# Where the first loads stand in an attention and mixture-of-experts kernel: weights loaded later, bias loads on another queue, and three PSUM banks in the first prologue

## The chip, the cores and the metric

The kernel runs on one core of a Trainium2 chip. The metric is the device time of one execution in microseconds (us); the time before is the median of three runs. One further execution was recorded by the profiler, and all times of single steps come from it.

## The reference

The input x has 8 batches of 1024 tokens with 256 features, all in float32. Two layers follow each other, each with a residual and a layer norm:

```
q, k, v = x Wq + bq, x Wk + bk, x Wv + bv               # 16 heads of 16
gate    = a (b c - 1) + 2,  a, b = sigmoid(sums of x gru_W + gru_b)
scores  = q k / 4 + gate[row] * rel_embed[bucket(col - row)][head]
x       = layernorm(x + softmax(scores) v Wo + bo)

p       = softmax(x Wr)                                  # 8 experts, best 2 per token
x       = layernorm(x + sum over the 2 experts of weight * ffn_e(x))
ffn(x)  = gelu(x W1 + b1) W2 + b2                        # 256 -> 1024 -> 256
```

An expert takes at most 2560 of the 8192 tokens, in their order; a token that meets a full expert goes through a fallback network instead.

## The kernel before

The program has two parts. The first does attention and routing for all batches, the second runs the experts over rows that the first part has scattered to DRAM. The change lies in the first part, before its main loop.

The main loop runs over units. A unit is a pair of heads of one batch, so there are 8 units per batch and 64 in all, with 16 steps each. A step takes 128 keys (j) and half of the queries (c): TensorE (PE) makes the scores, VectorE (DVE) adds the near part of the position bias, ScalarE (ACT) takes the exponential, and PE multiplies with v. To subtract a row's maximum beforehand, the kernel computes maxima of the scores in a pass of their own (`max_first`, `max_second`, `max_fold`), `LEAD` = 21 steps ahead of the scores. So 21 steps of maxima stand before the main loop: these are the "first maxima".

q and k are split into three bfloat16 parts each. `halves(b, xT, m)` does that for half m of the heads: for each half of the tokens a k projection and a q projection, four in all (four PE instructions each, called pq). ACT takes the first part out of PSUM (L626), DVE the remainder (L639), ACT the second part (L418), GpSimd (POOL) the third (L419), and a DMA on SyncE's queue stores the three to DRAM (`kd`, `qd`, L643; of k also differences, `dd`, L657). The SBUF tile `parts` has three buffers and is used by the gates too. `gating` computes the gates: two products pg, a bias added by DVE (z), a chain on ACT and POOL (g), two transposes pgt of it, and stores to `gd` and, in eight pieces each time, `fd` (L580, L591). `prologue` transposes x (pt, copied by ACT to xT, L468), starts `gating` and `halves(b, xT, 0)`, and makes v (pv). `load_unit` loads the parts of one unit back into ks, ks_d and qs: 19 DMAs per unit. `load_gates` loads a unit's gates (L965), which POOL multiplies with `bias` to `gb` (L985); `shift` stores a unit's maxima into qs (row, L1094).

These generators take turns in `streams`, a scheduler at build time: each says at a yield what it needs next. `BANK` takes the next entry of the list `banks`, a PSUM bank; after `HELD` or `SLOW` ACT or DVE reads that bank. Before the change the list has one entry, `(ps_x, "bank")`, until the last epilogue, where the banks `pm0` and `pm1` are added. These two otherwise hold the maxima.

The order of instructions on each engine has two regimes. From the line with `manual_schedule` (L393) on, each engine and queue takes them in the order in which the program states them. Before it a planner orders them by their readiness in its own estimate, and by their order in the program. So the tables and loads ahead of L393 need not run in the order of their lines.

The tables before the loop: from `embT` (the relative embeddings, transposed) DVE copies 79 pieces into `strip` (L318) and 79 into `back` (L325). `back` is stored to DRAM (`stripd`, L329), and one DMA of 4 MB spreads it to `blocks` (L332), from which each unit's `bias` is loaded (L950). DVE makes `strip16` from `strip`, stored as `stripb`, from which `biasb` is loaded (L929). `pattern` (ten loads) and zeros for `fd` (two stores of `zero`) come after them in the program.

The loads that the change touches: `heads_b` in DRAM gathers the small biases of k and q from five loads on ACT's queue; `bk_sb` and `bq_sb` are read back from it on ACT's queue (L230), and DVE scales `bq_sb` (L254). `later_weights`, called just before L393, loads on SyncE's (SP's) queue `wv_sb` (v projection), `wr_sb` (router), `bv_sb`, `bo_sb`, and `wo_sb` (output projection) in 16 pieces. The router's and the output projection's weights are read by `epilogue`, `bo_sb` by `add_bias`, all of it from batch 0's end on.

Of the kernel before, what the change touches and what calls it, by code (L numbers as in the profile page):

```python
# [11 lines left out]
F32 = mybir.dt.float32  # L12
# [4 lines left out]
ALU = mybir.AluOpType  # L17
# [4 lines left out]
P = 128  # L22
H, D = 16, 16
NG, HG = 4, 4
E = H * D
# [25 lines left out]
META = 5  # L51
# [27 lines left out]
def tile_attention_moe(  # L79
# [25 lines left out]
    nc = tc.nc  # L105
# [47 lines left out]
    with ExitStack() as at:  # L153
        cst = at.enter_context(tc.tile_pool(name="cst", bufs=1))
# [5 lines left out]
        ps_m = at.enter_context(tc.tile_pool(name="ps_m", bufs=1, space=PSUM))  # L160
        ps_x = at.enter_context(tc.tile_pool(name="ps_x", bufs=1, space=PSUM))
# [6 lines left out]
        banks = [(ps_x, "bank")]  # L168

        def bank(name):  # L170
            pool, tag = banks[0]
            banks.append(banks.pop(0))
            return pool.tile([P, CH], F32, tag=tag, name=name)
# [9 lines left out]
        def load_piece(b, n, tag="xp", bufs=3):  # L183

            xp = work.tile([P, 2, E], F32, tag=tag, name=f"xp{b}_{n}", bufs=bufs)
            nc.sync.dma_start(
                out=xp,
                in_=x[b, n * 2 * P : (n + 1) * 2 * P, :].rearrange(
                    "(t p) e -> p t e", p=P
                ),  # L190
            )
            return xp

        first_pieces = [load_piece(0, n) for n in range(3)]
        first_pieces.append(load_piece(0, 3, "rest", 2))


        emb = work.tile([NBUCKET, H], F32, tag="osb", name="emb", bufs=1)
        nc.sync.dma_start(out=emb, in_=rel)
# [2 lines left out]
            out=gb_ld.rearrange("p g o -> p (g o)"), in_=gru_b.to_broadcast([P, 8])  # L202
# [7 lines left out]
        bq_sb = cst.tile([P, NK], F32, name="bq_sb")  # L210
        bk_sb = cst.tile([P, NK], F32, name="bk_sb")
        for sb, src in ((wk_sb, wk), (wq_sb, wq)):
            for k in range(NK):
                nc.scalar.dma_start(
                    out=sb[:, k, :].rearrange("p (h d) -> p h d", d=D),
                    in_=src[k * P : (k + 1) * P, :].rearrange("p (h w) -> p h w", w=32)[
                        :, :, :D
                    ],
                )
        heads_b = dram.tile([2, H, D], F32, name="heads_b")  # L220
        nc.scalar.dma_start(
            out=heads_b[0], in_=kcl[8, :].rearrange("(h w) -> h w", w=32)[:, :D]
        )
        for g in range(H // HG):
            nc.scalar.dma_start(
                out=heads_b[1, g * HG : (g + 1) * HG, :],
                in_=bq[:, g].rearrange("(r w) -> r w", w=32)[:HG, :D],
            )
        for sb, which in ((bk_sb, 0), (bq_sb, 1)):
            nc.scalar.dma_start(  # L230
                out=sb,
                in_=heads_b[which].rearrange("h d -> (h d)").rearrange("(k p) -> p k", p=P),
            )
        wv_sb = cst.tile([P, NK, E], F32, name="wv_sb")
        wr_sb = cst.tile([P, NK, NE], F32, name="wr_sb")
        wo_sb = cst.tile([P, NK, E], F32, name="wo_sb")
# [1 line left out]
        bv_sb = cst.tile([P, E], F32, name="bv_sb")  # L238

        def later_weights():  # L240
            for sb, src in ((wv_sb, wv), (wr_sb, wr)):
                nc.sync.dma_start(out=sb, in_=src.rearrange("(k p) m -> p k m", p=P))
            nc.sync.dma_start(out=bv_sb, in_=bv.to_broadcast([P, E]))
            nc.sync.dma_start(out=bo_sb, in_=wo[D : D + 1, :].to_broadcast([P, E]))
            for h in range(H):
                k, r = divmod(h * D, P)
                nc.sync.dma_start(
                    out=wo_sb[r : r + D, k, :], in_=wo[h * 32 : h * 32 + D, :]
                )


        scale = 1.0 / math.sqrt(D)
        nc.vector.tensor_scalar(wq_sb, wq_sb, scale, None, ALU.mult)
        nc.vector.tensor_scalar(bq_sb, bq_sb, scale, None, ALU.mult)  # L254


        gs = cst.tile([P, 2], F32, name="gs")
# [8 lines left out]
        for base, sign in ((0, 1), (D - 1, -1)):  # L266
            nc.gpsimd.affine_select(
                out=wg, in_=wg, compare_op=ALU.is_ge, fill=0.0, base=base,
# [7 lines left out]
            out=anti, in_=anti, compare_op=ALU.not_equal, fill=1.0, base=-(P - 1),  # L276
# [7 lines left out]
            out=later, in_=later, compare_op=ALU.is_gt, fill=0.0, base=0,  # L284
# [5 lines left out]
            out=sel, in_=sel, compare_op=ALU.not_equal, fill=1.0, base=0,  # L290
# [32 lines left out]
        for lo, hi in zip(cuts[:-1], cuts[1:]):  # L323
# [9 lines left out]
            out=blocks,  # L333
            in_=bass.AP(
                sd.tensor, sd.offset + EDGE + 1 - REACH, [[STRIP, H], [-1, P], [1, WIN]]
            ),
# [15 lines left out]
        for side, bk in enumerate((int(farn[0]), int(far[0]))):  # L352
            nc.sync.dma_start(
                out=farb[:, side, :], in_=rel[bk : bk + 1, :].to_broadcast([P, H])
            )

        zero = cst.tile([P, 1, E + META], F32, name="zero")
        nc.gpsimd.memset(zero, 0.0)

        gd = [dram.tile([H, N], F32, name=f"gd{i}") for i in range(2)]  # L360
        qd = [dram.tile([3, E, N], BF16, name=f"qd{i}") for i in range(2)]
# [6 lines left out]
        for t in fd:  # L368
# [4 lines left out]
                out=flat, in_=zero16.unsqueeze(1).to_broadcast([P, flat.shape[1], 2 * E])  # L373
# [15 lines left out]
        o_acc = ps_o.tile([P, CH], F32, name="o_acc")  # L389
        nc.vector.memset(o_acc, 0.0)  # L390

        later_weights()
        at.enter_context(tc.manual_schedule())  # L393


        def clearing():
            for rows in (xd[:, :], yd[1:, :]):
                per, width = rows.shape[0] // P, rows.shape[1]
                spread = rows.rearrange("(p n) e -> p n e", p=P)
                for lo in range(0, per, 4):  # L400
                    n = min(4, per - lo)
                    nc.sync.dma_start(
                        out=spread[:, lo : lo + n, :],
                        in_=zero[:, :, :width].to_broadcast([P, n, width]),
                    )
                    for _ in range(4):
                        yield
            nc.sync.dma_start(out=yd[0:1, :], in_=zero[0:1, 0, :E])
# [46 lines left out]
        def prologue(b, pieces):  # L455
            me = batches[b]
            xT = once.tile([P, NK, N], F32, tag="xT", name=f"xT{b}")
            for n in range(NI // 2):
                yield BANK
                pt = bank("pt")  # L460
                ptv = pt.rearrange("p (k t n) -> p k t n", k=NK, t=2)
                for k in range(NK):
                    for t in range(2):
                        nc.tensor.transpose(
                            ptv[:, k, t, :], pieces[n][:, t, k * P : (k + 1) * P], ident
                        )
                yield HELD
                nc.scalar.copy(  # L468
                    xT[:, :, n * 2 * P : (n + 1) * 2 * P],
                    pt.rearrange("p (k n) -> p k n", k=NK),  # L470
                )
                if len(pieces) < NI // 2:
                    pieces.append(load_piece(b, len(pieces)))

            streams.start(gating(b, xT))
            yield from halves(b, xT, 0)


            v = perb.tile([P, NI, H, D + 1], F32, tag="v", name=f"v{b}")
            me.v = v  # L480
            nc.gpsimd.memset(v[:, :, :, D : D + 1], 1.0)
            for j in range(0, NI, 2):
                yield BANK
                pv = bank("pv")
                pvv = pv.rearrange("p (j e) -> p j e", j=2)
                for jj in range(2):
                    for k in range(NK):
                        nc.tensor.matmul(
                            pvv[:, jj, :],
                            xT[:, k, (j + jj) * P : (j + jj + 1) * P],  # L490
                            wv_sb[:, k, :],
                            start=(k == 0),
                            stop=(k == NK - 1),
                        )
                yield SLOW
                for jj in range(2):
                    nc.vector.tensor_tensor(
                        v[:, j + jj, :, 0:D],
                        pvv[:, jj, :].rearrange("p (h d) -> p h d", h=H),
                        bv_sb.rearrange("p (h d) -> p h d", h=H),  # L500
                        ALU.add,
                    )
            yield from halves(b, xT, 1)
# [552 lines left out]
        def max_second(m, common=False):  # L1056

            pm = bank("pm") if common else ps_m.tile([P, CH], F32, tag="pm0", name="pm0")
            half_scores(m, 0, pm)
            units[m // STEPS].rest = pm  # L1060
# [201 lines left out]
            load_max_bias(u)  # L1262
        load_bias(0)
        batches[0].rows, batches[0].gated = 0, False
        streams.start(prologue(0, first_pieces))
        while batches[0].rows < P or not batches[0].gated:
            streams.step()
# [1 line left out]
            nc.gpsimd.tensor_copy(t[R_FAR:], pattern[R_FAR:])  # L1269
        for t in KD:  # L1270
            nc.gpsimd.memset(t[R_FAR:], 0.0)
        clear = clearing()
        for u in range(2):
            for which in range(3):
# [4 lines left out]
        for m in range(LEAD):  # L1279
# [8 lines left out]
            streams.bank()  # L1288
            max_second(m)
        streams.drain()  # L1290
        for j in range(2):
            gate_biases(0, j)
        G = UNITS * STEPS
# [22 lines left out]
        for g in range(G + 12):  # L1316
            u, s = divmod(g, STEPS)
            j, c = divmod(s, NCH)
            b, sb = divmod(g, UB * STEPS)
            m = g + LEAD  # L1320
# [54 lines left out]
                take_outputs(u - 1)  # L1375
            next(clear, None)

        banks += [(ps_m, "pm0"), (ps_m, "pm1")]
        streams.start(epilogue(B - 1, batches[B - 1]))
        streams.drain()  # L1380

# [261 lines left out]
```

## Time and profile before

| | |
|---|---|
| median of three runs | 3657.59 us (3646.69 to 3658.37) |
| profiled execution | 3654.03 us, its span 3652.2 us |
| busy share of the span | PE 90%, POOL 61%, ACT 56%, DVE 53% |
| mean granted clock of PE | 0.963 |
| start of the first maximum (first L1025 on PE) | 101.04 us |
| start of the first scores of the main loop (L1109) | 140.03 us |
| PE busy from 0 to 101 us | 38.4 us |
| PE busy from 300 to 2426 us | 1991.7 us |

The span is the time from the first to the last instruction of the profiled execution; the execution's own time is 1.8 us longer. In a line of the order of time stand the start in us, the duration in us (of all instructions merged into the line), the engine, the line of the program, the operation, what it writes and reads, and the count; in brackets the idle time of the engine before it and what ended that. "SPq" and "ACTq" are the queues on which SP and ACT issue DMAs: the duration there is that of issuing, and the data lands later. A line of waits gives the waiting engine and line, whom it waited for, the total in us, how often, and the longest. A line of the stretches gives the stretch, its length, and the busy time of PE, PE's weight loads, DVE, ACT and POOL (in brackets the number of instructions), then PE's granted clock, the share of the DMA engines' time and GB/s.

### The profile page before, as it was taken

What the parts mean: (1) busy time and instruction counts of PE and PEld (TensorE: products, weight loads), DVE (VectorE), ACT (ScalarE), POOL (GpSimd) and SP (SyncE); (2) the same over time, 40 slices, a digit from 0 to 9 for tenths busy, and PEclk for the clock granted to TensorE, in tenths of its full rate; (3) what the DMA queues carried; (4) which work ended last, traced back from release to release, by engine and by line L of the source; (5) the groups of instructions that cost most, each with busy time, mean ns of one, the idle gap of its engine ahead of it and who ended that gap; (6) DMA issues with size and microseconds to landing.
All of it is one profiled execution on the core that took longest, in us unless ns stands there. A gap on an engine that the chain in (4) does not pass through costs nothing. (4 is left out here: it accounts for less than half of the span.)

```text
span 3652.2 us, 53430 instructions
## 1 busy us (share of the span) xinstructions
PE 3277.1 (90%) x16263; PEld 1655.8 (45%) x16263; DVE 1935.0 (53%) x5559; ACT 2047.8 (56%) x3084; POOL 2221.9 (61%) x2619
## 2 busy tenths in 40 slices
PE   4798998989999999999999999994399999999997
PEld 2342343334334334334334433333267677667776
DVE  2455656655765665665666576661134344444443
ACT  1577777767777777777787777771022222222222
POOL 2667666876886887787787788782233333333332
PEclk8899999999999999999999999995699999999999
DMA  5567657655643453444444444420332332232220
GB/s 139 159 167 196 190 167 192 186 177 177 186 146 111 139 155 114 130 141 135 125 135 137 133 135 129 132 92 10 113 88 58 88 90 67 85 96 88 72 90 21
DMA packets 380418, 455.71 MB, mean 125 GB/s; under 512 B 87478, under 2 KB 285235, under 8 KB 380107
## 3 DMA queue, kind: packets, MB, share of 16 engines
q1 hardware_dynamic: 338602, 388.06, 35.9%
q0 software_dynamic: 19296, 43.38, 4.2%
q10 hardware_dynamic: 22208, 20.58, 1.9%
q8 instruction: 138, 2.26, 0.3%
q14 instruction: 174, 1.42, 0.1%
HBM read 315.16 MB, written 140.54 MB: 125 GB/s over the span
## 5 line engine op out<-in xcount | busy, mean ns | idle before, releaser
L1131 ACT ACTIVATE pr<-sc 128x1024 f32<-128x1024 f32 x1024 | 1049.0, 1025 | 321.5 <-DVE sc L1124 298.9
L985 POOL TENSOR_TENSOR gb<-bias,gates 128x1024 f32<-128x1024 f32 (+2 forms) x512 | 1070.2, 2091 | 133.6 <-DMA gates<-gd 67.3
L1066 DVE CUSTOM_DVE_ANT_0 over<-pm,over 128x512 f32<-128x512 f32 x1024 | 703.8, 687 | 794.4 <-ACT over L1054 303.9
L1054 ACT ACTIVATE over<-pm 128x512 f32<-128x512 f32 x1024 | 612.7, 598 | 260.9 <-PE pm L1029 242.1
L1109 PE MATMUL sc<-qs,ks 122*128 122x512 bf16 x2048 | 617.4, 382 | 39.2 <-ACT pr L1131 24.7
L1124 DVE TENSOR_TENSOR sc<-sc,gb 128x640 f32<-128x640 f32 (+3 forms) x768 | 599.6, 781 | 77.6 <-POOL gb L985 56.0
L1029 PE MATMUL pm<-biasb,dgb 128*128 128x320 bf16 (+2 forms) x2048 | 579.2, 283 | 0.0
L1139 PE MATMUL o_acc<-pr,v 128*17 128x512 f32 x4096 | 551.9, 610 | 0.3 <-ACT pr L1131 0.3
L1481 PE MATMUL ph<-xsT,w 128*128 128x512 f32 (+1 forms) x1440 | 488.8, 497 | 13.3 <-ACT xsT L1421 12.7
L1496 PE MATMUL py<-w,hT 128*128 128x256 f32 x2208 | 485.0, 379 | 5.5 <-DVE ys L1503 5.5
L1496 PEld LDWEIGHTS py<-w,hT 128*128 128x128 f32 x2208 | 419.2, 190 | 74.1 <-issue 10.5
L1025 PE MATMUL pm<-ks,qs 120*128 120x512 bf16 x1024 | 396.5, 387 | 44.8 <-DVE mh L1066 25.7
L1025 PEld LDWEIGHTS <-qs 120*128 120x128 bf16 x2048 | 207.3, 101 | 505.2 <-issue 339.6
L1025 PE MATMUL pm<-ks_d,qs 120*128 120x512 bf16 x1024 | 393.9, 385 | 39.3 <-DMA qs<-qd 18.0
L1488 ACT ACTIVATE hT<-ph,b_sb 128x512 f32<-128x512 f32 (+1 forms) x360 | 212.3, 590 | 287.9 <-PE ph L1481 264.1
L1481 PEld LDWEIGHTS ph<-xsT,w 128*128 128x128 f32 x1440 | 270.7, 190 | 213.8 <-issue 169.1
L1421 ACT COPY xsT<-pt 128x512 f32<-128x512 f32 (+1 forms) x90 | 39.6, 490 | 567.5 <-PE pt L1418 567.5
L143 POOL TENSOR_TENSOR rs<-rstd,neghalf 128x1 f32<-128x1 f32 x138 | 78.3, 568 | 446.8 <-DVE rstd L141 446.4
L1029 PEld LDWEIGHTS <-dgb 128*128 128x128 bf16 x2048 | 201.7, 98 | 262.5 <-issue 147.2
L998 POOL TENSOR_TENSOR dgb<-anti,grev 128x256 bf16<-128x256 f32 x512 | 313.8, 613 | 4.9
L1109 PEld LDWEIGHTS <-ks 122*128 122x128 bf16 x2048 | 197.5, 99 | 221.4 <-issue 70.4
L419 POOL TENSOR_TENSOR parts<-rest,parts 128x512 bf16<-128x512 f32 (+1 forms) x80 | 92.5, 1157 | 239.7 <-ACT parts L418 193.4
(184 smaller groups left out, 2913.3 us busy)
## 6 DMA issues: line engine op xcount, KB each, us to landing
gates<-gd SPq DMA_DIRECT2D x128, 704.0 KB
biasb<-stripb SPq DMA_DIRECT2D x128, 288.0 KB
bias<-blocks SPq DMA_DIRECT2D x64, 512.0 KB
xd<-zero SPq DMA_DIRECT2D x51, 522.0 KB
ks<-kd SPq DMA_DIRECT2D x384, 64.0 KB
qs<-qd SPq DMA_DIRECT2D x384, 64.0 KB
yd<-zero SPq DMA_DIRECT2D x40, 512.0 KB
w<-in_w_dram ACTq DMA_DIRECT2D x16, 1024.0 KB
```

Of the source, the lines that this page charges most:

```text
L985: nc.gpsimd.tensor_tensor(gb_[:, :, off : off + hi - lo], me.bias[:, :, off : off + hi - lo], gates[:, :, lo - at : hi - at], ALU.mult,)
L998: nc.gpsimd.tensor_tensor(dg, anti.unsqueeze(1).to_broadcast([P, HP, P]), batches[b].grev[:, i, hp * HP : (hp + 1) * HP] .unsqueeze(2) .to ...
L1025: nc.tensor.matmul(pm, QS[u % 3][:R_SHIFT, h, i * P : (i + 1) * P], keys, start=True, stop=False)
L1029: nc.tensor.matmul(pm[:, lo:hi, :], dgb[m - h][:, h, :], me.biasb[:, at : at + (hi - lo) * P].rearrange("p (j n) -> p j n", n=P)[:, :, :HALF],
L1054: nc.scalar.activation(me.over, pm, AF.Relu)
L1066: nc.vector.tensor_tensor_reduce(out=me.over, in0=me.rest, in1=me.over, scale=1.0, scalar=-3.0e38, op0=ALU.add, op1=ALU.max, accum_out=me. ...
L1109: nc.tensor.matmul(me.sc[:, h, :], ks[:, h, j * P : (j + 1) * P], qs[:, h, c * CH : (c + 1) * CH], start=True, stop=True,)
L1124: nc.vector.tensor_tensor(sc[:, :, lo - c * CH : hi - c * CH], sc[:, :, lo - c * CH : hi - c * CH], me.gb[j][:, :, off : off + hi - lo], A ...
L1131: nc.scalar.activation(pr, sc, AF.Exp)
L1139: nc.tensor.matmul(o_acc[r : r + D + 1, :], batches[b].v[:, j, hp * HP + h, :], prs[c][:, h, :], start=(j == 0), stop=(j == NI - 1),)
L1481: nc.tensor.matmul(ph[:, :size], w1_sb[:, k, f * P : (f + 1) * P], xsT[:, k, :size], start=(k == 0), stop=(k == NK - 1),)
L1496: nc.tensor.matmul(py, hT[:, f, t * P : (t + 1) * P], w2_sb[:, f, :], start=(f == 0), stop=(f == NF - 1),)
```

## The change

There are four edits, all in the first part.

1. The loads of `bk_sb` and `bq_sb` move from ACT's queue to SP's queue, and in the program from behind the `heads_b` loads to behind `farb`. The scaling of `bq_sb` on DVE moves from behind that of `wq_sb` to just before `later_weights`.
2. `later_weights` keeps `wv_sb` and `bv_sb`. The loads of `wr_sb`, `bo_sb` and the 16 of `wo_sb` go to a new function, `last_weights`, called behind the loop of the 21 first maxima and ahead of the main loop. They stay on SP's queue.
3. `pm0` and `pm1` are in the list `banks` while batch 0's prologue runs up to its first half and its gates; after that the list is the single bank again.
4. The tile `zero` is made and cleared at the beginning instead of behind `farb`.

```
+        zero = cst.tile([P, 1, E + META], F32, name="zero")
+        nc.gpsimd.memset(zero, 0.0)
...
-        for sb, which in ((bk_sb, 0), (bq_sb, 1)):
-            nc.scalar.dma_start(
-                out=sb,
-                in_=heads_b[which].rearrange("h d -> (h d)").rearrange("(k p) -> p k", p=P),
-            )
...
         def later_weights():
-            for sb, src in ((wv_sb, wv), (wr_sb, wr)):
-                nc.sync.dma_start(out=sb, in_=src.rearrange("(k p) m -> p k m", p=P))
+            nc.sync.dma_start(out=wv_sb, in_=wv.rearrange("(k p) m -> p k m", p=P))
             nc.sync.dma_start(out=bv_sb, in_=bv.to_broadcast([P, E]))
+
+        def last_weights():
+            nc.sync.dma_start(out=wr_sb, in_=wr.rearrange("(k p) m -> p k m", p=P))
             nc.sync.dma_start(out=bo_sb, in_=wo[D : D + 1, :].to_broadcast([P, E]))
             for h in range(H):
...
-        nc.vector.tensor_scalar(bq_sb, bq_sb, scale, None, ALU.mult)
...
-        zero = cst.tile([P, 1, E + META], F32, name="zero")
-        nc.gpsimd.memset(zero, 0.0)
+        for sb, which in ((bk_sb, 0), (bq_sb, 1)):
+            nc.sync.dma_start(
+                out=sb,
+                in_=heads_b[which].rearrange("h d -> (h d)").rearrange("(k p) -> p k", p=P),
+            )
...
+        nc.vector.tensor_scalar(bq_sb, bq_sb, scale, None, ALU.mult)
         later_weights()
...
+        own_banks = [(ps_m, "pm0"), (ps_m, "pm1")]
+        banks += own_banks
         streams.start(prologue(0, first_pieces))
         while batches[0].rows < P or not batches[0].gated:
             streams.step()
...
+        banks = [(ps_x, "bank")]
         clear = clearing()
...
         streams.drain()
+        last_weights()
         for j in range(2):
             gate_biases(0, j)
...
-        banks += [(ps_m, "pm0"), (ps_m, "pm1")]
+        banks += own_banks
         streams.start(epilogue(B - 1, batches[B - 1]))
```

## The prediction

> **What bounds the kernel now.** I read the page first: PE is busy 90% of the span, in the 2,286 us of attention main loop after 140 us and in the experts after it. The diff touches neither, only what precedes the main loop, so I read the stretches, then the waits, then SyncE's (SP's) own queue. Two of the stretches:
>
> ```profile
> 0.00:101.00 101.00, 38.43 (x99) 22.23 (x99) 23.37 (x189) 14.73 (x27) 28.02 (x51) 0.85 0.53 138
> ...
> 300.00:2426.00 2126.00, 1991.66 (x11043) 800.30 (x11041) 1346.85 (x3252) 1603.84 (x2342) 1639.11 (x1911) 0.98 0.50 149
> ```
>
> In the first 101 us, up to the first maxima, PE (first column) works 38 us and no engine more: this stretch is latency. The waits of 0 to 140 us name the gaps:
>
> ```profile
> ACT parts L626 <- DMA kd<-parts: 15.6, 1, 15.6
> ...
> PE pm L1025 <- DMA ks<-kd: 9.9, 1, 9.9
> ...
> DVE bq_sb L254 <- DMA bq_sb<-heads_b: 7.9, 1, 7.9
> ```
>
> ACT waits 15.6 us for a buffer of parts (three of them) whose store has not landed. Why the store is late stands in SP's order of time:
>
> ```profile
> 33.26 0.32 SPq L329 DMA_DIRECT2D stripd<-back  x1
> ...
> 35.27 0.59 SPq L332 DMA_DIRECT2D blocks<-stripd  x1
> ...
> 44.12 3.11 SPq L243 DMA_DIRECT2D bv_sb<-in_bv_dram  x1
> 54.08 0.35 SPq L244 DMA_DIRECT2D bo_sb<-in_wo_dram  x1
> 54.47 7.37 SPq L247 DMA_DIRECT2D wo_sb<-in_wo_dram  x16
> 61.88 1.96 SPq L929 DMA_DIRECT2D biasb<-stripb  x4
> 63.89 0.69 SPq L950 DMA_DIRECT2D bias<-blocks  x1
> 64.67 0.50 SPq L643 DMA_DIRECT2D kd<-parts  x1
> ```
>
> The data of that kd store was ready at 42.3 us (POOL's L419), but it went out at 64.67 and released ACT at 72.83. Ahead of it stand the 4 MB blocks transfer, for whose landing bo's issue waited 6.8 us (SP's waits: "L244 <- DMA blocks"), though bo reads nothing of it: bo is the eighth issue behind blocks, so SP lets eight transfers be open at once. Then come 16 issues for wo. And blocks was late because DVE was:
>
> ```profile
> 20.03 0.37 ACTq L230 DMA_DIRECT2D bq_sb<-heads_b  x1
> 20.43 1.28 ACT L468 ACT_TABLE_LOAD   x1 [20.43 <-DMA pattern<-in_kcr_dram]
> ...
> 23.84 0.17 DVE L254 TENSOR_SCALAR bq_sb<-bq_sb 128x2 f32<-128x2 f32 x1 [7.92 <-DMA bq_sb<-heads_b]
> 23.92 3.86 DVE L318 COPY strip<-embT 16x1 f32<-16x1 f32 x57
> ...
> 27.71 5.53 DVE L325 COPY back<-embT 16x205 f32<-16x205 f32 x79
> ```
>
> DVE stood 7.92 us before bq's scaling with 136 copies behind it; the last gives stripd, and so blocks. The path is: bq, copies, stripd, blocks, wo's issues, kd's store, the fourth projection (q of the second half), gates' stores, unit 0's loads, first maximum at 101.04.
>
> **The change part by part.** The sum is made against the profiled execution's 3654.0 us (span 3652.2, 1.8 around it); the median of the three runs is 3657.6, 3.6 above it, and they spread from 3646.7 to 3658.4. About 0.3%, 11 us, is what a measurement can tell from no change.
>
> *Small biases' loads on SP, bq's scaling last on DVE.* DVE's 22 copies ended at 15.92; without the wait the rest takes 3.86 + 5.53 = 9.4 us, so back ends at 25.3 instead of 33.24: -7.9 us for stripd, if SP is free then. SP loses at the new waits: bq's issue on ACT could not go before 20.03 (heads_b's four loads land late), so SP stands until 20.4, with pattern, fd, stripd and the kd stores queued behind. It idled until 18.19 anyway, on heads_b ("L382", 7.8 us). Seven pattern and fd issues took it from 18.19 to 23.4; from 20.4 on they end at 25.6, at stripd's new time. Were all twelve put ahead, stripd would go at 29, 3.5 us worse; were the biases behind stripd, nothing is lost. I take 0 and keep 3.5. bq's load landed 3.4 us after its issue, at about 24; DVE reaches the scaling after the strip16 pair (0.51 + 0.87 us) at 26.7, so it does not stand there.
> ACT loses its two issues and starts its table load at about 14 instead of 20.43, so xT comes 6.4 us sooner; that is not on the path, since the fourth projection waits for the store anyway. zero's memset (0.31 us of POOL) moves where POOL idles 11.7 us: 0.
>
> *Router and output weights behind the first maxima.* With blocks issued at 27.4 and 18.8 us until landing (35.27 to 54.08), it lands at 46.2. Then bo and wo, 61.88 - 54.08 = 7.8 us, are gone; wr's 1.26 us lay inside the wait for blocks: 0. biasb and bias are still ahead of kd; bias reads blocks, so it cannot pass. So kd goes out 7.9 + 7.8 = 15.7 us earlier, at 49.0, and frees the buffer at 57.1 instead of 72.83. biasb might go out before the landing: up to 2.8 us better.
>
> *Three PSUM banks in turns.* Until that buffer comes free PE is not late: from 13.33 the four transpose groups (1.12 us each), two pg (3.59) and four pq (3.78) take 27 us at the rate of these rows, and DVE, free at 27, lets the second pq start at about 29; the fourth is done near 41, 16 us before its reader can start. So most of what the banks save there is lost: 0. Behind it they count. Before: from ACT's start at 72.83 to POOL's last parts of the gates, 86.45, are 13.6 us, because pgt, pv, pgt each waited for DVE to empty the one bank. With both pgt and a pv in other banks, what is left is ACT and DVE in line: ACT 0.69 + 0.40, q's cast 0.62 after DVE's 0.75 (by 2.1 us), gT and parts 1.15, DVE rest 0.68, cast 0.62, gT and parts 1.15, rest 0.68, cast 0.62, POOL 1.15: 8.3 us with the hand-overs. Gain 5.3 us (bounds 0 and 7). From there to the first maximum the SP issues fd, ks, ks_d, qs run as before, 14.6 us.
>
> *What moves in.* wr, bo and wo go out behind the last of the 21 first maxima, where SP ends qs<-row at 136.7: 0.35 + 7.37 + about 0.7 = 8.4 us ahead of bias, the clears, biasb, unit 2's loads and these:
>
> ```profile
> 154.84 0.38 SPq L965 DMA_DIRECT2D gates<-gd  x1
> ...
> 161.97 1.91 SPq L1094 DMA_DIRECT2D qs<-row  x2
> ```
>
> POOL already waited 4.1 us for these gates, starting unit 1's gb at 159.84, ready at 161.4; the DVE add that needs it came at 168.7, a cover of some 7 us. SP idles 156.3 to 162.0, so the qs row goes at most 2.7 us late. Cost between 0 and 8.4; I take 3, the cover's shortfall and the row's delay. wo itself is read only in batch 1.
>
> Sum: -7.9 - 7.8 - 5.3 + 3 = -18 us: 3636.0 on the profiled execution, 3639.6 on the median. I give 3637.
>
> *A rule weighed.* The row: kd's store, behind 1.7 MB of biasb and bias on its own queue, took 8.2 us to land, while stripd on an empty queue let blocks go 2.0 us after it. So if the planner puts the bias loads behind blocks, they land at 46, not 24. The Trainium skill's "DMA: Bandwidth & Descriptors", section "Queues, rings and completion order", speaks against the change here: SP and ACT each own a ring on every DMA engine, a ring is served in order, and engines take turns between rings, so a load taken off ACT's ring loses its own turn. By that rule the sum would be the first rival's.
>
> **The rivals.**
> - *Biases behind blocks.* ACT's first k parts then start at 46.5; q's projection waits for z behind bq's scaling (46.8), and the chain of pq at 3.78 us with DVE's reads gives the fourth at 59 instead of 57.1, 2.5 us worse with kd's store: 3639.5. For it: they stand in one queue. Against: in the program they stand ahead of the pattern loads, of which five went out before stripd. 0.10.
> - *The banks bring nothing* behind the fourth projection, because SP's stores of fd (two times 3.6 us) are the limit: 3642. 0.10.
> - *The weights' 8.4 us count whole* at the main loop's head: 3642.5. For it: POOL's wait for gates. 0.14.
> - *The front is swallowed.* Stripd at 29, no gain of the banks and the weights' 8.4 us whole: -21 + 3.5 + 5.3 + 8.4 = -4: 3650. 0.10.
> - *Slower:* the moved issues keep SP behind for good, so each unit's gates and rows come 8.4 us late, through the four units in which batch 1's stores share the queue: 34 us lost against 21 gained, 3667. It decides if SP idles under 8.4 us per unit; it idled 5.7 + 8.9 us in two gaps alone between 156 and 202, which speaks against. 0.06.
>
> Forecast: 0.50.
>
> **How the numbers follow.** The forecast's bounds downwards are 2.8 (biasb sooner), 1.7 (banks) and 3 (no cost of the moved issues), 7.5 together, and upwards 3.5 (stripd) and 5.4 (8.4 instead of 3), 8.9; with some 6 us of spread between runs on either side that is 3623 to 3652, which holds the first four rivals too. Faster by over 11 us (below 3646.6): 0.44 of the forecast's 0.50, 0.25 of the next three rivals' 0.34, 0.02 of the swallowed front: 0.71. Same: what is left of these, 0.22. Slower: the last rival and what I don't see, 0.07.
>
> **What would show it.** In the changed profile: back ending near 25.3 and blocks issued near 27.4; kd's first store near 49 and the fourth projection's parts near 57; ACT's table load near 14; 8 us between that parts and POOL's last gates' parts; the first maximum near 80; 18 issues on SP near 115 and unit 1's gates behind them; the main loop's length unchanged within some 5 us. Wrong would be: stripd or the bias loads held on SP, a first maximum later than 90, or a first unit longer by over 8 us.

## The result, and the profile after

The changed kernel takes 3644.0 us (median of 20 runs) where the kernel before takes 3654.6 us (20 runs): the ratio is 0.997, 95% interval 0.9962 to 0.9978. The forecast was 3637 us, from a sum of 18 us less than before; 10.6 us came. The profiled execution has a span of 3638.0 us against 3652.2 us, 14.2 us less.

The front of the kernel moved as forecast, almost to the microsecond. The order of time on ACT and DVE, the lines that answer to DVE's wait and to the late table load:

```profile
12.73 6.36 DVE L317 COPY strip<-embT 16x205 f32<-16x205 f32 x79
...
12.99 1.28 ACT L471 ACT_TABLE_LOAD   x1 [12.99 <-DMA heads_b<-in_bq_dram]
...
19.02 5.54 DVE L324 COPY back<-embT 16x205 f32<-16x205 f32 x79
...
25.72 0.15 DVE L394 TENSOR_SCALAR bq_sb<-bq_sb 128x2 f32<-128x2 f32 x1
...
55.14 0.69 ACT L629 ACTIVATE parts<-pq,bq_sb 128x512 bf16<-128x512 f32 x1 [20.34 <-DMA kd<-parts]
```

All 158 copies run in one piece, and bq's scaling comes behind them without a wait. ACT still stands for the store that frees parts, but until 55.14 instead of 72.83. SP's own order of time shows why:

```profile
24.90 0.31 SPq L328 DMA_DIRECT2D stripd<-back  x1
...
27.03 0.59 SPq L331 DMA_DIRECT2D blocks<-stripd  x1
...
36.86 10.42 SPq L932 DMA_DIRECT2D biasb<-stripb  x4
47.32 0.47 SPq L953 DMA_DIRECT2D bias<-blocks  x1
47.89 0.41 SPq L646 DMA_DIRECT2D kd<-parts  x1
```

stripd goes out 8.4 us sooner. What now waits for the landing of blocks is the second of the four biasb issues, the eighth issue behind blocks: SP's waits give it 7.9 us, and the four took 10.42 us where they took 1.96 before. The store for parts comes behind them. The first maximum starts at 80.18 us instead of 101.04, the first scores of the main loop at 117.48 instead of 140.03: 22.5 us sooner. But unit 0's outputs leave PSUM at 158.8 instead of 172.0, only 13.2 sooner. The unit is 9.4 us longer. SP's order at the head of the main loop:

```profile
115.09 0.57 SPq L243 DMA_DIRECT2D wr_sb<-in_wr_dram  x1
115.71 0.46 SPq L244 DMA_DIRECT2D bo_sb<-in_wo_dram  x1
116.22 8.23 SPq L247 DMA_DIRECT2D wo_sb<-in_wo_dram  x16
124.49 0.42 SPq L953 DMA_DIRECT2D bias<-blocks  x1
...
138.11 3.08 SPq L918 DMA_DIRECT2D qs<-qd  x6
141.93 0.38 SPq L968 DMA_DIRECT2D gates<-gd  x1
```

Everything behind the 18 moved issues is 9 to 10 us later against the main loop (gates 24.5 us behind the first scores instead of 14.8). Who waits for it, from the waits of 117 to 158 us:

```profile
POOL biasb L946 <- DMA biasb<-stripb: 8.4, 1, 8.4
PE pm L1028 <- DMA qs<-qd: 8.0, 1, 8.0
POOL gb L988 <- DMA gates<-gd: 6.9, 1, 6.9
```

PE, the busiest engine here, stands 8.0 us for the qs load of unit 2. POOL's two waits held up no other engine: none is listed as waiting for POOL from 117 to 159 us. From unit 0's outputs to the last unit's outputs the two profiles need the same: 2299.8 us before and 2300.4 after.

### The profile page after: what moved, and what is told of

Same layout as the page of the kernel before. It is cut to its first block, busy times and chain, and to the rows that moved or that the text cites. A ratio compares the mean times of both kernels' runs of the same rounds, so it can differ in the third digit from the quotient of the medians.

```text
span 3638.0 us, 53431 instructions
## 1 busy us (share of the span) xinstructions
PE 3266.2 (90%) x16263; PEld 1651.2 (45%) x16263; DVE 1926.7 (53%) x5559; ACT 2043.5 (56%) x3084; POOL 2225.2 (61%) x2619
## 5 line engine op out<-in xcount | busy, mean ns | idle before, releaser
L1523 POOL DMA_INDIRECT out_dram<-o,dst_i x138 | 145.4, 1054 | 154.3 <-DVE o L145 71.4
```

## The experiments

The theory, with its parts: the front gained by DVE's wait, wo's issues and the banks, and 9.4 us of it were lost in unit 0 to SP's queue. The milestones of all profiles, in us ("parts" is ACT's start on the fourth projection, "outputs" the time at which a unit's sums leave PSUM; each row is one profiled execution):

| | parts | first maximum | first scores | unit 0's outputs | last outputs | span |
|---|---|---|---|---|---|---|
| before | 72.83 | 101.04 | 140.03 | 172.0 | 2471.8 | 3652.2 |
| after | 55.14 | 80.18 | 117.48 | 158.8 | 2459.2 | 3638.0 |
| 1 weights spread | 55.31 | 80.81 | 117.68 | 148.9 | 2455.4 | 3634.0 |
| 2 biasb first | 55.41 | 81.49 | 119.78 | 158.7 | 2461.1 | 3640.5 |
| 3 as 1, one bank | 54.62 | 83.60 | 122.70 | 154.7 | 2456.0 | 3635.7 |
| 4 biases alone | 65.49 | 94.03 | 131.74 | 162.9 | 2467.3 | 3646.2 |
| 5 weights alone | 61.77 | 90.02 | 127.04 | 158.3 | 2462.9 | 3640.7 |
| 6 banks alone | 73.00 | 98.47 | 136.19 | 167.4 | 2461.9 | 3641.4 |
| 7 biases behind blocks | 59.45 | 84.72 | 123.84 | 155.8 | 2471.2 | 3651.0 |
| 8 tables later | 47.92 | 76.85 | 114.57 | 145.8 | 2444.9 | 3626.3 |
| 9 both places | 48.64 | 75.03 | 112.75 | 144.0 | 2456.2 | 3636.6 |
| after, again | 55.82 | 81.25 | 118.96 | 161.0 | 2468.7 | 3648.9 |
| before, again | 72.31 | 100.58 | 139.62 | 171.6 | 2487.6 | 3666.6 |

**1. The moved loads spread over later steps.** `last_weights` becomes a generator that yields behind each issue:

```
-        last_weights()
+        moved = last_weights()
...
+            if g >= 18 and g % 2 == 0:
+                next(moved, None)
```

> The changed kernel, but the 18 moved loads (router, output projection's bias and weights) go out one per two steps from step 18 of the main loop on, instead of all ahead of it. Theory A: the 9.4 us that they hold SP's queue at the main loop's head are lost in unit 0 (its outputs came 41.3 us after the first scores instead of 31.9). Then the first maximum and the first scores stay at 80.2 and 117.5 us, unit 0's outputs come at 149 to 151 instead of 158.8, and the time falls by 9 us below the changed kernel's: 0.994 to 0.995 of before. Theory B: unit 0 is longer because PE's clock or the phase of the pipeline differs at its new place, not because of the queue. Then unit 0's outputs stay near 158 and the ratio near 0.997.

Measured: 3634.8 us (median of 6 runs), ratio to before 0.9954, interval 0.9937 to 0.9971. The first scores stay at 117.68 and unit 0's outputs come at 148.9. The stretch from the first scores to the outputs, of the changed kernel and of this one:

```profile
117.48:158.80 41.32, 32.95 (x180) 11.86 (x178) 21.41 (x50) 27.19 (x37) 25.09 (x21) 0.88 0.68 168
```

```profile
117.68:148.90 31.22, 30.67 (x181) 11.53 (x179) 21.41 (x50) 26.96 (x38) 25.06 (x21) 1.00 0.79 203
```

The same instructions on the same engines take 10.1 us less once SP has nothing in the way: theory A. The time alone does not decide it, since its interval holds the ratios of both theories. PE's own busy time is also 2.3 us less, at a granted clock of 1.00 instead of 0.88: right behind the stand of 8 us the same eight o_acc instructions took 1.91 us instead of 1.05. The spreading has a price of its own: the stretch between unit 2's and unit 3's outputs is 50.6 us, where the changed kernel needs 47.8, at the same granted clock of 0.93.

**2. biasb ahead of the moved loads.** Of three waits, one taken away:

```
+        load_max_bias(2)
         last_weights()
...
-                    if s == 1:
+                    if s == 1 and u:
                         load_max_bias(u + 2)
```

> The changed kernel, but unit 2's biasb load (two issues) goes out ahead of the 18 moved loads; everything else stays behind them. Theory A1: what costs unit 0 its 9.4 us is unit 2's qs load, the last of 19 behind the moved ones, for which PE stood 8.0 us. Then POOL's wait for biasb (8.4 us) goes and unit 0's outputs still come 40 to 42 us after the first scores. Theory A2: POOL's wait for biasb holds up gb and dgb, and the wait for qs is only its shadow. Then unit 0 takes 32 to 34 us.

Measured: unit 0 takes 38.9 us from first scores to outputs, between the two expectations and nearer to A1's 40 to 42. POOL's wait for biasb is gone, and PE still stands for qs:

```profile
PE pm L1028 <- DMA qs<-qd: 5.4, 1, 5.4
```

So PE's wait for unit 2's qs is no shadow of POOL's. It is 2.6 us shorter than in the changed kernel, and so is the unit by 2.4: with two issues fewer between the moved ones and qs, the last qs issue ends 21.5 us behind the first scores instead of 23.7. POOL still stands, 12.0 us, ahead of unit 1's gb. With 1, where nothing stands ahead of qs and PE has no such wait left, the late qs load is the cause.

**3. One bank, weights spread.** Run 1 without the third edit.

```
-        banks += own_banks
         streams.start(prologue(0, first_pieces))
```

> As the first run, but with one PSUM bank in the first prologue as before the change. The prediction's step: the banks gain nothing until the fourth projection and 5.3 us behind it. Then that projection's parts stay within 1 us of 55.1, POOL's last parts of the gates come 13 to 14 us after it instead of 8.2, and the first maximum at 85 to 86. Rival: the two times eight fd issues are the limit behind it, and the banks bring nothing: first maximum at 80 to 81.

Measured: parts at 54.62, as expected; POOL's last parts of the gates start at 67.51 instead of 62.34:

```profile
67.51 1.15 POOL L424 TENSOR_TENSOR parts<-rest,parts 48x512 bf16<-48x512 f32 x1 [6.50 <-ACT parts L423]
```

That is 5.2 us, where the prediction had 5.3. But the first maximum comes at 83.60, only 2.8 us later than with three banks, not 5: with three banks SP's two times eight fd issues end later than POOL's data is ready, so the rival was half right. The first scores are 5.0 us later; the other 2.2 us arise in the first maxima, which ran at a granted clock of 0.85 here and 0.96 in run 1; what sets the clock there is open.

**4, 5 and 6. Each edit alone.** The kernel before with the first and fourth edit; with the moved loads alone, spread as in 1; and with the banks alone.

> The kernel before, with the first and fourth edit alone (bias loads on SP's queue, bq's scaling last on DVE, zero early); weights and single bank as before. Theory (the prediction's first term): the 7.9 us of DVE's wait are passed on whole along back, stripd, blocks, the 16 issues of wo and kd's store: stripd near 25.3, first store near 57, the fourth projection's parts near 65, the first maximum at 93 instead of 101.0. Rival: the 7.9 us are taken up at the next wait (the bias loads hold SP, or blocks lands no sooner because the queue's other transfers share the engines), and the first maximum comes at 97 or later.

> The kernel before, with the weights moved alone (one issue per two steps from step 18 of the main loop on); bias loads on ACT's queue and one bank as before. Theory (the second term): only what stood behind the landing of blocks counts, 7.8 us: stripd stays at 33.3, the first store goes out near 56.9, the fourth projection's parts come near 65, the first maximum at 93. Rival: SP was not what held the store, since blocks and biasb fill the same rings, and the parts come at 69 or later.

> The kernel before, with the three banks alone. Theory (the third term): nothing until the fourth projection, whose parts stay at 72.8; behind it 5.2 us less to POOL's last parts of the gates (86.45 less 5.2 is 81.2), of which SP's two times eight fd issues leave some 3 at the first maximum: 98. Rival: PE, freed from waiting for readers, keeps its full clock from 15 us on and the whole front is sooner: parts before 70, first maximum before 94.

Measured at the first maximum: the biases 7.0 us sooner, the weights 11.0, the banks 2.6. Together 20.6, and the whole change 20.9: the parts add up. The weights gave 3.2 us more than expected. SP's order of time at that place, weights alone:

```profile
42.18 11.84 SPq L933 DMA_DIRECT2D biasb<-stripb  x4
54.07 0.47 SPq L954 DMA_DIRECT2D bias<-blocks  x1
54.63 0.41 SPq L647 DMA_DIRECT2D kd<-parts  x1
```

The store goes out at 54.63, not 56.9. Three things make up the 3.2 us. First, stripd was 1.2 us sooner in that run (32.05 us, 33.26 before), since bq's load kept DVE 6.73 us instead of 7.92. Second, the first of the biasb issues now goes out while SP waits for blocks anyway (the second is the one that waits): from blocks landing to the store's issue it was 10.6 us before (54.08 to 64.67) and is 1.8 now by an estimate (blocks goes out at 34.06, with the 18.8 us of before that is 52.9), 8.8 less where 7.8 had been expected. Third, the store landed 7.1 us behind its issue instead of 8.2. With the banks alone the parts stay at 73.0 and POOL's last parts end at 81.18, the expected 81.2. PE did run the last two of the four projections at twice the earlier rate with three banks (four pq instructions in 1.97 and 1.88 us instead of 3.78 and 3.65), but the fourth one's reader waits for the store, so the rival fell.

**7. The bias loads behind blocks.** On the kernel of run 1, they move behind `later_weights`, with the scaling:

```
         at.enter_context(tc.manual_schedule())
+        for sb, which in ((bk_sb, 0), (bq_sb, 1)):
+            nc.sync.dma_start(
...
+        nc.vector.tensor_scalar(bq_sb, bq_sb, scale, None, ALU.mult)
```

> As the first run (moved loads spread from step 18 on), but the loads of bk and bq go out on SP's queue behind wv and bv, and so behind blocks, near 36 us, and bq's scaling behind them on DVE. The first rival of the prediction. Theory: a load behind a 4 MB transfer on one queue lands when that has landed: ACT's first k parts start at 46 to 47 instead of 20.6 us, bq (the eighth issue behind blocks) goes out only then and lands at 48 to 50, q's projection follows, and the fourth projection's parts come at 60 to 63 instead of 55.3, the first maximum at 85 to 89 instead of 80.8. Other outcome: small loads pass the big one and bk lands within 3 us of its issue; then the first parts start at 39 to 40, the fourth projection's stay at 55 and the first maximum at 81.

Measured, the issue on SP and the start on ACT:

```profile
36.93 2.14 SPq L393 DMA_DIRECT2D bk_sb<-heads_b  x1
46.77 0.38 SPq L393 DMA_DIRECT2D bq_sb<-heads_b  x1
```

```profile
48.03 0.69 ACT L630 ACTIVATE parts<-pq,bk_sb 128x512 bf16<-128x512 f32 x1 [30.78 <-DMA bk_sb<-heads_b]
```

A load of 1 KB landed about 11 us after its issue, when the 4 MB ahead of it had landed, and the first maximum came 3.9 us later than in run 1, at 84.72, just under the 85 to 89 expected. This is the first rival of the prediction as a kernel; its price was put at 2.5 us. By the Trainium skill's "DMA: Bandwidth & Descriptors", section "Queues, rings and completion order", a ring is served in order; this run agrees, with the 11 us. In the changed kernel the planner put both loads at 16.8 and 19.6 us, ahead of blocks, so the rule did not bite.

**8. The tables later.** Run 1, with biasb and bias behind the third store of parts (`stored` is a list that gets an entry at each store):

```
-        for u in range(2):
-            load_max_bias(u)
-        load_bias(0)
+        late = True
...
             streams.step()
+            if late and len(stored) == 3:
+                late = False
+                for u in range(2):
+                    load_max_bias(u)
+                load_bias(0)
```

> As the first run, and the loads of biasb for units 0 and 1 and of bias for unit 0 go out behind the third store of parts (k, q, k) instead of ahead of the first. Theory: the first store waits only because bias reads blocks and stands ahead of it; without that it goes out near 36 us and lands with blocks near 47, the fourth projection's parts come at 47 to 49 instead of 55.1, the first maximum at 72 to 74 instead of 80.2, and the time falls by 6 to 8 us more: 0.992 to 0.993 of before. Rival: the store's data stands in the queue's rings behind biasb or blocks anyway, and SP's later issues become the limit: first maximum at 78 to 81, no change of time against the first run.

Measured: 3630.7 us (median of 6 runs), ratio 0.9945, interval 0.9928 to 0.9961, where 0.992 to 0.993 had been expected. It is the lowest median here, though its interval overlaps that of run 1. The store's issue, and ACT behind it:

```profile
36.29 1.01 SPq L649 DMA_DIRECT2D kd<-parts  x1
...
46.29 0.44 SPq L649 DMA_DIRECT2D qd<-parts  x1
46.83 0.47 SPq L649 DMA_DIRECT2D kd<-parts  x1
47.35 2.93 SPq L939 DMA_DIRECT2D biasb<-stripb  x4
```

```profile
47.92 0.69 ACT L631 ACTIVATE parts<-pq,bq_sb 128x512 bf16<-128x512 f32 x1 [12.09 <-DMA kd<-parts]
```

ACT's parts come 7.4 us sooner than in run 1, as the theory said. Only 4.0 us of it are left at the first maximum (76.85, expected 72 to 74), because the tables now stand ahead of the first eight fd issues, which took 7.24 us instead of 3.61.

**9. Both places changed.** Run 8, with unit 0's bias behind its gates (not shown), and the moved loads, but for bo, in units 4 to 7.

```
-            if g >= 18 and g % 2 == 0:
+            if g == 40 or g >= 66 and g % 3 == 0:
```

> As the run with the tables later, with two more places changed: bias for unit 0 goes out behind unit 0's gates, and of the moved loads only bo's goes out early (step 40), the rest one per three steps from step 66 on, in the units that have no prologue of the next batch. Theory: in the first run the moved loads, spread over units 1 to 3, cost unit 3 some 4 us (50.6 between its outputs and the unit's before instead of 46.3), because SP is short of time there; in the later units it has time to spare. Then that unit takes 46 to 47 us, units 4 to 7 stay at 30 to 33, the first maximum comes at 75 to 77, and the time falls 3 to 5 us below the run with the tables later: ratio 0.993 to 0.994. Rival: unit 3 is longer for another reason, such as PE's clock in it, and stays near 50.

Measured: the stretch to unit 3's outputs is 47.4 us instead of 50.9, at a granted clock of 0.93 in both, so the clock is not the reason; 46 to 47 had been expected. The first maximum comes at 75.03, as expected. But the time is 3635.2 us (6 runs, ratio 0.9955, interval 0.9936 to 0.9973), not the 3 to 5 us below run 8's. The stretches of units 4 to 7 are 34.6, 34.1, 31.3 and 34.3 us, with a clock under 1.00 in three of them, against 32.4, 33.2, 30.7 and 30.7 in run 8. Whether the moved loads or chance did that is open.

**10 and 11. Both kernels once more.** Unchanged, for a second profile each.

> The changed kernel once more, unchanged, for a second profile. The units of the main loop differ between the profiles by 1.5 to 4 us where PE's granted clock in them is 0.95 or 0.90 instead of 1.00. Theory: where these stretches of half clock fall is chance of each execution. Then the first maximum (80.2), the first scores (117.5) and unit 0's outputs (158.8) repeat within 1 us, and units 3 to 7, which took 34.3, 34.2, 32.0, 30.4 and 34.2 us, come with another pattern of clocks and lengths. Rival: the pattern belongs to the kernel; then the same units show 0.90 to 0.95 and the same lengths.

> The kernel before once more, unchanged, for a second profile. As for the changed kernel: by the theory of chance the first maximum (101.0), the first scores (140.0) and unit 0's outputs (172.0) repeat within 1 us, and the units at a clock under 1.00 (among units 1 to 16: 1, 3, 5, 8, 11, 12, 15, 16) are partly others, each 1.5 to 2.5 us longer than at 1.00. By the rival they are the same ones.

Measured: the first maximum, the first scores and unit 0's outputs of the kernel before repeat within 0.5 us, those of the changed kernel within 1.1 to 2.2, where 1 had been expected. The loss in unit 0 repeats as well: 42.0 us from first scores to outputs at a granted clock of 0.88, with PE standing 8.4 us for qs. The length of the rest does not repeat. From unit 0's outputs to the last, the kernel before took 2299.8 us in one execution and 2316.0 in the other. One of its units, from output to output, in the first profile and in the second:

```profile
637.90:669.60 31.70, 30.21 (x181) 11.66 (x180) 20.98 (x58) 24.95 (x35) 25.07 (x41) 1.00 0.61 191
```

```profile
642.00:675.70 33.70, 31.81 (x181) 11.99 (x180) 21.00 (x58) 25.01 (x35) 25.66 (x44) 0.95 0.59 182
```

The same 181 PE instructions at a granted clock of 0.95 take 1.6 us more of PE, and the unit 2.0 us more. Summed over the main loop's units, the time not granted is 37 us in the first profile (unit length by one less the clock) and 50 us in the second, 13 us more. PE's busy time over the same stretch is 2143.1 and 2151.3 us, 8.1 more. So about half of the 16 us shows in slower PE instructions; how much of the other half comes from the clock is not shown. Of the 19 units under 1.00 in the first profile, 15 are under 1.00 in the second too (among them units 1, 3, 11 and 12), and 8 others join them: most of the pattern belongs to the kernel, as the rival said, and a part to the single execution.

The Trainium skill's "TensorE: Matmul & The Clock Gate", "Part 1: The HAM clock gate", says that the clock is halved after an idle window of some 3.4 us and given back after a busy one, and that the windows run freely, not from the kernel's start. In the second profile's unit the loss lies in one stretch of that length:

```profile
661.00:664.50 3.50, 3.50 (x15) 0.88 (x14) 0.59 (x2) 1.78 (x3) 0.17 (x1) 0.51 1.01 293
```

So the trace agrees with the half and with the window's length. It does not show the idle window: the one wait of PE in this unit, for a qs load just ahead of that stretch, was 1.5 us long. Why the clock fell there stays open.

## Why the prediction was right or wrong

The mechanism of the front was right: it is a chain of waits, and 21 us of it went. That something comes back from the moved issues was right too, but not which wait brings it back, nor how much. The sum of 18 us was too large by 7 because of that one term. The time came 7 us above the forecast; that it is no farther off was in part luck, since two other errors of about 3 us each cancel.

- *Bias loads and bq's scaling, -7.9:* alone 7.0 at the first maximum. back ended at 24.6 (25.3 said), stripd's place on SP was kept, and bq's load was there in time. blocks took 19.6 us until SP went on in that run instead of 18.8: most of the missing microsecond.
- *The weights on the front, -7.8:* alone 11.0. Of the 3.2 us more, 1.2 belong to that run (bq's load came sooner), 1.0 is the one biasb issue that passes before blocks has landed, and 1.0 the store's shorter flight (7.1 us instead of 8.2; in the changed kernel 7.25, from 47.89 to 55.14). The prediction kept 2.8 us as a bound for issues that go out ahead of the landing; 1.0 of it came.
- *The banks, -5.3:* behind the fourth projection exactly that (8.2 us to POOL's last parts instead of 13.6), but 2.6 at the first maximum. The step that failed is "From there to the first maximum the SP issues fd, ks, ks_d, qs run as before, 14.6 us": the first eight fd issues end later than POOL's last data, so SP begins the second eight 1.8 us late. This error and the one before it cancel.
- *What moves in, +3:* 9.4 in unit 0. This is the step that was mis-sized. The issues were put at 8.4 us of SP and were 9.4, but the step went wrong in its choice of who waits. It took the cover of the gates (7 us) and of the qs row. It named unit 2's loads among what comes later, but gave them no price, though they stand ahead of the gates in the same queue. The last of them and unit 2's first maximum, which needs it, in the trace of before:

```profile
150.97 3.09 SPq L915 DMA_DIRECT2D qs<-qd  x6
...
158.99 0.38 PE L1025 MATMUL pm<-ks_d,qs 120*128 120x512 bf16 x1
```

and that maximum in the changed kernel:

```profile
143.74 0.58 PE L1028 MATMUL pm<-ks_d,qs 120*128 120x512 bf16 x1 [7.96 <-DMA qs<-qd]
```

In the trace of before the last issue ended at 154.06, 4.9 us ahead of PE's start. In the changed kernel, where PE waited, 2.55 us passed from the end of the last issue (141.19) to PE's start, so the cover was 4.9 - 2.55 = 2.4 us. 9.7 us of delay against the main loop less 2.4 is 7.3; PE stood 8.0. The rival "The weights' 8.4 us count whole" had the size right, and its 3642.5 us are nearer to the 3644.0 measured than the forecast; but it named POOL's wait for gates, and it was PE's for qs. The prediction's own sign of being wrong, a first unit longer by over 8 us, was met with 9.4.

- *Not in the sum:* the first maxima themselves, up to the first scores, took 37.3 us instead of 39.0, at a granted clock of 0.95 instead of 0.85 (37.7 and 39.0 in the second profiles). The change gained 1.7 us there without a term for it; why the clock was higher is open.
- *Slower for good:* no. Behind unit 0 the loop takes what it took.

With the front as measured and the term at 9.4 the sum is 20.9 - 9.4 = 11.5, or 13.2 with the first maxima, where the medians have 10.6. The 14.2 us between the two profiles cannot be told from either: single executions of one kernel differ by some 20 us (before 3644.6 to 3664.2, after 3633.6 to 3655.3 over 20 runs each).

## What to carry to other kernels

A transfer that nobody needs soon is not free at the place where it is put next: list what is queued behind it and compare each with the time at which its reader wants it; the tightest one sets the price, and it may be a load for work two units ahead. On a queue that serves in order, the load that releases a buffer should not stand behind one that must wait for a big transfer; moving two tables behind three stores brought 7.4 us to that buffer. When single edits are timed alone at a milestone inside the profile, they can be told apart by one or two microseconds where the whole time spreads by twenty.

## What the runs showed of the hardware

PE's granted clock in the main loop is not the kernel's alone: over the same 63 units the kernel before lost 37 us of granted time in one execution and 50 in the next, PE was busy 8.1 us more, and the loop was 16 us longer. A halved clock needs no long stand: a stretch of 3.5 us at 0.51 came behind a wait of 1.5 us. A stand of PE costs more than itself: in unit 0 of the changed kernel 8.0 us of waiting came with a granted clock of 0.88, and PE's busy time was 2.3 us more than without the wait. And at the beginning of the kernel the clock's record cannot be trusted: before the change it reads 1.00 for 14 to 57 us, while four pq instructions took 3.78 us there and 1.98 later; after it the same four took 1.9 us from 17 us on, except for one group at 3.6 us behind a wait of 4.75 us.
